# Heron's step for the reciprocal deviation, b2 moved between engines, and later loads, in a conditional residual adapter

## The chip, the cores and the metric

The kernel runs on one core of one Trainium2 chip. The metric is the device time of one execution in microseconds (us). Five engines of the core have queues of their own: TensorE (PE in the profile, and PEld for its weight loads), VectorE (DVE), ScalarE (ACT), GpSimd (POOL), and SyncE (SP), which here only issues DMAs. They run side by side and wait for each other through semaphores.

## What is computed

For each of 128 batches a language id picks one of ten sets of weights. With x of 128 rows and 512 columns per batch, all in fp32:

```python
h = jax.nn.relu(jnp.einsum('bsh,bha->bsa', x, W1[ids]) + b1[ids][:, None, :])   # 512 -> 128
adapted = jnp.einsum('bsa,bah->bsh', h, W2[ids]) + b2[ids][:, None, :]          # 128 -> 512
y = x + adapted
mean = jnp.mean(y, axis=-1, keepdims=True)
var = jnp.mean(jnp.square(y - mean), axis=-1, keepdims=True)
normed = (y - mean) * jax.lax.rsqrt(var + 1e-5)
out = x + normed * gamma[ids][:, None, :] + beta[ids][:, None, :]
```

## The kernel before

**Tiles.** One batch is one tile of 128 rows by 512 columns. x is loaded in groups of G = 4 batches (1 MB) into four buffers (`xp`). All of W1 and W2 stays in SBUF. At the start the ten rows of beta, gamma and b2 are spread over the 128 partitions by small products with a matrix `pick` of ones and zeros (`spread`), into `beta_b`, `gamma_b` and `b2_b`.

**One batch** goes through these steps. TensorE transposes x in four pieces into PSUM (`transpose_x`, L197) and ScalarE copies the result to SBUF (`copy_xT`, L201). ScalarE copies the batch's W1 into one of three buffers (`stage_w1`, L192). TensorE multiplies (`down`, L220), ScalarE applies b1 and relu (`relu`, L228), and TensorE multiplies by W2 (`up`, L237) into y, which has five PSUM buffers (`p_y`). VectorE adds the residual in place and takes the row sums (`residual`, L243), makes the negative mean (L248), later subtracts it and multiplies by gamma (`scale`, L287), and last multiplies by the reciprocal deviation and adds the rest (`finish`, L296), into `o`, which SyncE stores two batches at a time (`store`, L300). ScalarE takes the squares and their sum (`square`, L255) and, for two batches at a time, the root (`deviation`, L261).

**The reciprocal deviation** for two batches is made by five narrow VectorE operations, `rstd_1` to `rstd_5` (L266 to L281): the reciprocal of ScalarE's root, and one Newton step on it.

**b2 and beta.** GpSimd prepares x + b2 (`add_b2`, L207, into `r` of four buffers) and x + beta (`add_beta`, L214, into `o`). For the first four batches and each fourth after them (b % 4 == 1) TensorE adds b2 instead: `up` starts with a product of `pick` and the rows (L236), and the residual is x itself. So GpSimd has seven operations in four batches.

**The order** is written out by hand: the function `keep` ties each instruction to the one before it on its engine, so that each queue runs in program order. Iteration i transposes batch i, multiplies down batch i-1 and up batch i-2 (U = 2), and VectorE works on batch b = i-3 and the pair before it: in even b residual, scale, mean, `rstd_1`, `rstd_2`, finish of batch b-3, `rstd_3`; in odd b residual, `rstd_4`, scale, `rstd_5`, mean, finish of b-3. Each engine that needs language ids loads four of them into registers every fourth batch (`lid`, L174), ahead of use. The load of the group three ahead stands at the top of iterations with i % 4 == 0 (L462) and waits on SyncE's queue until all readers of its buffer are done. At the start up(2) is placed at i = 4 by hand (L465). The last four batches, 124 to 127, go through `tail`, which has an order of its own and gives part of the finish of three batches to ScalarE and GpSimd (`by_pool`); E = 123.

Of the kernel before, what the change touches and what calls it, by code (L numbers as in the profile page):

```python
# [8 lines left out]
FP = mybir.dt.float32  # L9
# [14 lines left out]
def cond_resid_kernel(ctx: ExitStack, tc: tile.TileContext, x, itok, W1, b1, W2, b2, gamma, beta, out):  # L24
# [45 lines left out]
    def xb(b):  # L70
        return xs[b // G][:, b % G, :]
# [55 lines left out]
    both = st.tile([P, R], FP, tag="both", name="both", bufs=1)[:96, :]  # L127
    keep(nc.vector.tensor_tensor(both, ident[:96, 0:R], ident[:96, 32 : 32 + R], ALU.add))
    keep(nc.vector.tensor_tensor(pick, both, ident[:96, 64 : 64 + R], ALU.add))


    wrap = const.tile([1, B], I32, name="wrap")
# [51 lines left out]
        return lids[g, engine][b % G]  # L184

    def b2_by_matmul(b):
        return b < 4 or b % 4 == 1

    def stage_w1(b):
        w1s[b] = wp.tile([P, KC, A], FP, tag="w1s", name=f"w1s_{b}")  # L190
# [10 lines left out]
        keep(nc.scalar.copy(xT[b], pxs.pop(b)))  # L201

    def add_b2(b):
        if not b2_by_matmul(b):
            rs[b] = rp.tile([P, H], FP, tag="r", name=f"r_{b}")
            v = lid(b, ET.Pool)
            keep(nc.gpsimd.tensor_tensor(rs[b], xb(b), b2_b[:, bass.ds(v * H, H)], ALU.add))  # L207
# [22 lines left out]
    def up(b):  # L230
# [6 lines left out]
        keep(nc.tensor.matmul(ys[b], lhsT=hT[b], rhs=w2[:, bass.ds(v * H, H)], start=not m, stop=True))  # L237
        del hT[b]

    def residual(b):  # L240
        r = xb(b) if b2_by_matmul(b) else rs.pop(b)
        s = st.tile([P, 1], FP, tag="sum", name=f"sum_{b}")
        keep(nc.vector.scalar_tensor_tensor(ys[b], ys[b], 1.0, r, ALU.mult, ALU.add, accum_out=s))  # L243
        sums[b] = s

    def negative_mean(b):
        nmeans[b] = st.tile([P, 1], FP, tag="nmean", name=f"nmean_{b}")
        keep(nc.vector.tensor_scalar(nmeans[b], sums.pop(b), -1.0 / H, None, ALU.mult))  # L248

    def square(b):  # L250
        g, j = divmod(b, 2)
        if j == 0:
            ssqs[g] = st.tile([P, 2], FP, tag="ssq", name=f"ssq_{g}")
        sq = tp.tile([P, H], FP, tag="sq", name=f"sq_{b}")
        keep(nc.scalar.activation(sq, ys[b], AF.Square, bias=nmeans[b], accum_out=ssqs[g][:, j : j + 1]))  # L255

    sds, y0s, stats = {}, {}, {}

    def deviation(g):
        sds[g] = st.tile([P, 2], FP, tag="sd", name=f"sd_{g}")  # L260
        keep(nc.scalar.activation(sds[g], ssqs[g], AF.Sqrt, bias=eps, scale=1.0 / H))  # L261


    def rstd_1(g):
        stats[g] = p_s.tile([P, 6], FP, tag="s", name=f"stat_{g}")
        keep(nc.vector.tensor_scalar(stats[g][:, 0:2], ssqs.pop(g), -0.5 / H, -0.5 * EPS, ALU.mult, ALU.add))  # L266

    def rstd_2(g):
        y0s[g] = st.tile([P, 2], FP, tag="y0", name=f"y0_{g}")
        keep(nc.vector.reciprocal(y0s[g], sds.pop(g)))  # L270

    def rstd_3(g):
        keep(nc.vector.tensor_tensor(stats[g][:, 2:4], stats[g][:, 0:2], y0s[g], ALU.mult))  # L273

    def rstd_4(g):
        keep(nc.vector.tensor_tensor(stats[g][:, 4:6], stats[g][:, 2:4], y0s[g], ALU.mult))  # L276

    def rstd_5(g):
        rstds[g] = st.tile([P, 2], FP, tag="rstd", name=f"rstd_{g}")
        keep(  # L280
            nc.vector.scalar_tensor_tensor(rstds[g], stats.pop(g)[:, 4:6], 1.5, y0s.pop(g), ALU.add, ALU.mult)  # L281
        )

    def scale(b):
        v = lid(b, ET.DVE)
        keep(
            nc.vector.scalar_tensor_tensor(  # L287
                ys[b], ys[b], nmeans.pop(b), gamma_b[:, bass.ds(v * H, H)], ALU.add, ALU.mult
            )
        )  # L290

# [11 lines left out]
    def on(b):  # L303
        return 0 <= b < B
# [6 lines left out]
    def rstd_of(b, n):  # L311

        if not ends:
            ends["t"] = p_s.tile([P, 32], FP, tag="s", name="stat_ends")
        t = ends["t"][:, 8 * (b % 4) : 8 * (b % 4) + 3]
        if n == 1:
            keep(nc.vector.tensor_scalar(t[:, 0:1], ssqs.pop(b), -0.5 / H, -0.5 * EPS, ALU.mult, ALU.add))  # L317
        elif n == 2:
            y0s[b] = st.tile([P, 1], FP, tag="y0", name=f"y0_{b}")
            keep(nc.vector.reciprocal(y0s[b], sds.pop(b)))  # L320
        elif n < 5:
            keep(nc.vector.tensor_tensor(t[:, n - 2 : n - 1], t[:, n - 3 : n - 2], y0s[b], ALU.mult))  # L322
        else:
            rstds[b] = st.tile([P, 1], FP, tag="rstd", name=f"rstd_{b}")
            keep(nc.vector.scalar_tensor_tensor(rstds[b], t[:, 2:3], 1.5, y0s.pop(b), ALU.add, ALU.mult))  # L325

    def deviation_of(b):
        ssq = st.tile([P, 1], FP, tag="ssq", name=f"ssq_{b}")
        sq = tp.tile([P, H], FP, tag="sq", name=f"sq_{b}")
        keep(nc.scalar.activation(sq, ys[b], AF.Square, bias=nmeans[b], accum_out=ssq))  # L330
        sds[b] = st.tile([P, 1], FP, tag="sd", name=f"sd_{b}")
        keep(nc.scalar.activation(sds[b], ssq, AF.Sqrt, bias=eps, scale=1.0 / H))
        ssqs[b] = ssq

    def rstd_col(b):
        return rstds[b] if b > E else rstds[b // 2][:, b % 2 : b % 2 + 1]

    def shift(b):
        ends[b] = st.tile([P, 1], FP, tag="shift", name=f"shift_{b}")
        keep(nc.vector.tensor_tensor(ends[b], nmeans.pop(b), rstd_col(b), ALU.mult))  # L340

    def by_pool(b, scaled):

# [16 lines left out]
    def tail(b):  # L360
        p = E // 2
        if b == E + 3:
            rstd_of(b - 2, 4)
        residual(b)
        if b == E + 1:
            rstd_1(p)
            rstd_2(p)
            negative_mean(b)
            rstd_3(p)
            scale(E - 1)  # L370
            rstd_4(p)
            rstd_5(p)
            shift(E)
            finish(E - 2)
            store(p - 1)
            deviation_of(b)
            by_pool(E, False)
        elif b == E + 2:
            negative_mean(b)
            rstd_of(b - 1, 1)  # L380
            rstd_of(b - 1, 2)
            finish_last(E - 1)
            store_last(E)
# [181 lines left out]
```

## Time and profile before

| | us |
|---|---|
| median of 3 runs (319.55 to 320.61) | 319.67 |
| the profiled execution | 319.72 |
| its span (first to last instruction) | 318.0 |
| TensorE multiplies, busy | 302.7 |
| VectorE, busy | 297.9 |
| ScalarE, busy | 289.1 |
| GpSimd, busy | 280.6 |

The granted TensorE clock is 0.99 of full speed in the mean. The profile holds each instruction with its start and duration. Records on VectorE, ScalarE and TensorE overlap with the next one, since an instruction can begin before its forerunner has written its last result; the time that one really takes up on its engine is therefore read from start to start. A line of a timeline gives start, duration, engine, line, operation, what is written and read, shapes, and in brackets the idle time before it with what ended it. A line of the waits gives who waited for whom, the total in us, how often, and the longest.

### The profile page before, as it was taken

The numbers are of one execution on the slowest core, as the hardware profiler recorded it, in microseconds if no ns is written. First come the engines' busy times: TensorE is split into PE (matmuls) and PEld (weight loads), VectorE is DVE, ScalarE is ACT, GpSimd is POOL, SyncE is SP. The second block draws the span as 40 slices with busy tenths as digits, with TensorE's granted clock in tenths as the row PEclk, the third lists the DMA queues.
The fourth block names the chain that finished last, engine by engine and source line by source line (L and its number), as shares of the span: only waits on it lengthen the run. The fifth ranks groups of instructions, "written<-read, shape, count | busy, mean of one in ns | idle before, by whom it ended". The sixth has DMA issues, their size and how long they took to land. (4 is left out here: it accounts for less than half of the span.)

```text
span 318.0 us, 7173 instructions
## 1 busy us (share of the span) xinstructions
PE 302.7 (95%) x1883; PEld 225.0 (71%) x1884; DVE 297.9 (94%) x995; ACT 289.1 (91%) x726; POOL 280.6 (88%) x234
## 2 busy tenths in 40 slices
PE   7989999999999999999999999999999999999950
PEld 3566777777777777777777777777777777777730
DVE  6827999999999999999999999999999999999995
ACT  3977999999999999999999999999999999999971
POOL 1308999999999999999999999999999999999873
PEclk9999999999999999999999999999999999999995
DMA  7998777667776666677776666677766666633333
GB/s 204 318 386 294 205 260 262 233 232 266 260 242 212 215 223 242 228 238 265 261 231 215 209 227 248 223 245 264 258 220 208 222 231 241 219 128 133 132 128 138
DMA packets 41002, 72.88 MB, mean 229 GB/s; under 512 B 1753, under 2 KB 6884, under 8 KB 40962
## 3 DMA queue, kind: packets, MB, share of 16 engines
q1 hardware_dynamic: 40902, 72.38, 67.2%
q8 instruction: 15, 0.25, 0.3%
q14 instruction: 25, 0.20, 0.2%
q10 hardware_dynamic: 60, 0.05, 0.1%
HBM read 38.86 MB, written 33.55 MB: 228 GB/s over the span
## 5 line engine op out<-in xcount | busy, mean ns | idle before, releaser
L214 POOL TENSOR_TENSOR o<-x,beta_b 128x512 f32<-128x512 f32 x128 | 162.1, 1280 | 9.2 <-ACT beta_b L164 9.2
L207 POOL TENSOR_TENSOR r<-x,b_b 128x512 f32<-128x512 f32 x93 | 118.9, 1279 | 20.2 <-DMA x<-in_x_dram 12.3
L220 PE MATMUL ph<-xT,w1s 128*128 128x128 f32 x1024 | 135.6, 275 | 0.7 <-ACT w1s L192 0.5
L237 PE MATMUL py<-w,hT 128*128 x256 | 131.0, 594 | 0.9 <-DMA w<-in_L_cond_W_dram 0.7
L220 PEld LDWEIGHTS ph<-xT,w1s 128*128 128x128 f32 x1024 | 124.6, 192 | 2.8 <-ACT hT L228 1.4
L197 PEld LDWEIGHTS pxT<-ident,x 128*128 128x128 f32 x512 | 63.7, 140 | 66.1 <-issue 45.3
L287 DVE SCALAR_TENSOR_TENSOR py<-py,nmean,gamma_b 128x512 f32<-128x512 f32 x126 | 94.6, 751 | 0.0
L255 ACT ACTIVATE sq<-py,nmean 128x512 f32<-128x512 f32 x124 | 85.3, 688 | 6.7 <-DVE nmean L248 4.2
L296 DVE SCALAR_TENSOR_TENSOR o<-py,rstd,o 128x512 f32<-128x512 f32 x122 | 90.3, 740 | 1.0
L192 ACT COPY w1s<-w 128x512 f32 x128 | 79.5, 622 | 0.2 <-DMA w<-in_L_cond_W_dram 0.2
L201 ACT COPY xT<-pxT 128x512 f32<-128x512 f32 x128 | 73.8, 577 | 5.1 <-PE pxT L197 3.6
L197 PE MATMUL pxT<-ident,x 128*128 128x128 f32 x512 | 76.8, 273 | 0.7 <-ACT xT L201 0.7
L243 DVE SCALAR_TENSOR_TENSOR py<-py,r 128x512 f32<-128x512 f32 x93 | 64.4, 692 | 2.5 <-PE pxT L197 0.9
L228 ACT ACTIVATE hT<-ph,b1T 128x128 f32<-128x128 f32 x128 | 47.6, 372 | 1.2 <-PE ph L220 1.2
L237 PEld LDWEIGHTS py<-w,hT 128*128 128x128 f32 x256 | 41.6, 192 | 4.0 <-issue 2.0
L243 DVE SCALAR_TENSOR_TENSOR py<-py,x 128x512 f32<-128x512 f32 x35 | 24.1, 690 | 4.9 <-PE py L237 4.8
L255 ACT ACTIVATION_READ_ACCUMULATOR sq<-py,nmean 128x1 f32 x124 | 24.8, 200 | 0.0
L261 ACT ACTIVATE sd<-ssq,eps 128x2 f32<-128x2 f32 x62 | 18.3, 296 | 2.1
L248 DVE TENSOR_SCALAR nmean<-sum 128x1 f32<-128x1 f32 x128 | 18.7, 146 | 0.2
L236 PE MATMUL py<-parts,pick 96*128 96x512 bf16 x35 | 13.3, 381 | 0.0
L243 DVE DVE_READ_ACCUMULATOR py<-py,r 128x1 f32 x93 | 13.0, 140 | 0.0
L276 DVE TENSOR_TENSOR stat<-stat,y 128x2 f32<-128x2 f32 x62 | 12.7, 205 | 0.0
(54 smaller groups left out, 113.7 us busy)
## 6 DMA issues: line engine op xcount, KB each, us to landing
out_dram<-o SPq DMA_DIRECT2D x61, 512.0 KB, 3.6
x<-in_x_dram SPq DMA_DIRECT2D x30, 1024.0 KB, 6.0
w<-in_L_cond_W_dram SPq DMA_DIRECT2D x4, 640.0 KB, 6.6
w<-in_L_cond_W_dram SPq DMA_DIRECT2D x2, 1280.0 KB, 11.3
x<-in_x_dram SPq DMA_DIRECT2D x4, 512.0 KB, 8.5
out_dram<-o SPq DMA_DIRECT2D x6, 256.0 KB, 2.4
rows<-in_L_cond_beta_dram ACTq DMA_DIRECT2D x1, 20.0 KB
rows<-in_L_cond_gamma_dram SPq DMA_DIRECT2D x1, 20.0 KB
```

The costliest lines, as they stand in the source:

```text
L192: keep(nc.scalar.copy(w1s[b].rearrange("p k a -> p (k a)"), src))
L197: keep(nc.tensor.transpose(pxs[b][:, k, :], xb(b)[:, k * P : (k + 1) * P], ident))
L201: keep(nc.scalar.copy(xT[b], pxs.pop(b)))
L207: keep(nc.gpsimd.tensor_tensor(rs[b], xb(b), b2_b[:, bass.ds(v * H, H)], ALU.add))
L214: keep(nc.gpsimd.tensor_tensor(os[g][:, j, :], xb(b), beta_b[:, bass.ds(v * H, H)], ALU.add))
L220: nc.tensor.matmul(phs[b], lhsT=w1s[b][:, k, :], rhs=xT[b][:, k, :], start=(k == 0), stop=(k == KC - 1))
L228: keep(nc.scalar.activation(hT[b], phs.pop(b), AF.Relu, bias=b1T[:, bass.ds(lid(b, ET.Activation), 1)]))
L237: keep(nc.tensor.matmul(ys[b], lhsT=hT[b], rhs=w2[:, bass.ds(v * H, H)], start=not m, stop=True))
L243: keep(nc.vector.scalar_tensor_tensor(ys[b], ys[b], 1.0, r, ALU.mult, ALU.add, accum_out=s))
L255: keep(nc.scalar.activation(sq, ys[b], AF.Square, bias=nmeans[b], accum_out=ssqs[g][:, j : j + 1]))
L287: nc.vector.scalar_tensor_tensor(ys[b], ys[b], nmeans.pop(b), gamma_b[:, bass.ds(v * H, H)], ALU.add, ALU.mult)
L296: nc.vector.scalar_tensor_tensor(o, ys.pop(b), rstds[g][:, j : j + 1], o, ALU.mult, ALU.add)
```

## The change

- **The reciprocal deviation** takes four narrow operations in place of five. With s the root and v the variance (each with its constants), it forms 1/s, v/s, v/s + s, and the reciprocal of that, which is half of the wanted 1/deviation; the factor 2 goes into gamma, by doubling gamma's columns of `pick` once at the start. `square` computes (sum - 512 y)^2, so its bias is the sum and not the mean; the constants of the root follow (1/H^3).
- **The order of VectorE's narrow operations**: `rstd_1` moves ahead of scale in even batches, `rstd_5` and its place are gone, so that `rstd_4` stands ahead of scale in odd ones. `tail` is ordered anew.
- **b2**: batches with b % 8 == 5 from 13 to 109 no longer have it from TensorE; VectorE adds it to y in place with a tensor_tensor ahead of the residual. GpSimd's share is unchanged.
- **Loads of x** stand at b % 4 == 0, three iterations later, when their buffer is free.
- **up(3)** is issued at the top of iteration 5, ahead of transposes(5) and down(4), in place of its end.
- The last additions of GpSimd, after batch 123, alternate.
- Sums and means of two batches share a tile.

```diff
+    keep(nc.vector.tensor_scalar(pick[:, L : 2 * L], pick[:, L : 2 * L], 2.0, None, ALU.mult))
...
     def b2_by_matmul(b):
-        return b < 4 or b % 4 == 1
+        return b < 4 or (b % 4 == 1 and not b2_by_vector(b))
+
+    def b2_by_vector(b):
+        return b % 8 == 5 and 8 <= b < B - 16
...
     def residual(b):
...
+        if b2_by_vector(b):
+            v = lid(b, ET.DVE)
+            keep(nc.vector.tensor_tensor(ys[b], ys[b], b2_b[:, bass.ds(v * H, H)], ALU.add))
+        keep(
+            nc.vector.scalar_tensor_tensor(ys[b], ys[b], 1.0, r, ALU.mult, ALU.add, accum_out=col(sums, b))
+        )
...
     def square(b):
...
-        keep(nc.scalar.activation(sq, ys[b], AF.Square, bias=nmeans[b], accum_out=ssqs[g][:, j : j + 1]))
+        keep(
+            nc.scalar.activation(
+                sq, ys[b], AF.Square, bias=col(sums, b), scale=-float(H), accum_out=col(ssqs, b)
+            )
+        )
...
     def rstd_1(g):
+        y0s[g] = p_s.tile([P, 6], FP, tag="s", name=f"stat_{g}")
+        keep(nc.vector.reciprocal(y0s[g][:, 0:2], sds[g]))
 
     def rstd_2(g):
+        t = y0s[g]
+        keep(nc.vector.scalar_tensor_tensor(t[:, 2:4], ssqs.pop(g), EPS * H3, t[:, 0:2], ALU.add, ALU.mult))
 
     def rstd_3(g):
+        t = y0s[g]
+        keep(nc.vector.scalar_tensor_tensor(t[:, 4:6], t[:, 2:4], 1.0 / H3, sds.pop(g), ALU.mult, ALU.add))
 
     def rstd_4(g):
         rstds[g] = st.tile([P, 2], FP, tag="rstd", name=f"rstd_{g}")
+        keep(nc.vector.reciprocal(rstds[g], y0s.pop(g)[:, 4:6]))
...
     def tail(b):
         p = E // 2
         if b == E + 3:
-            rstd_of(b - 2, 4)
+            rstd_of(b - 2, 3)
         residual(b)
         if b == E + 1:
             rstd_1(p)
+            scale(E - 1)
             rstd_2(p)
             negative_mean(b)
-            rstd_3(p)
-            scale(E - 1)
-            rstd_4(p)
-            rstd_5(p)
-            shift(E)
             finish(E - 2)
             store(p - 1)
+            rstd_3(p)
             deviation_of(b)
+            rstd_4(p)
+            shift(E)
             by_pool(E, False)
         elif b == E + 2:
+            rstd_of(b - 1, 1)
             negative_mean(b)
-            rstd_of(b - 1, 1)
             rstd_of(b - 1, 2)
             finish_last(E - 1)
             store_last(E)
-            rstd_of(b - 1, 3)
             deviation_of(b)
         elif b == E + 3:
-            rstd_of(b - 2, 5)
-            negative_mean(b)
+            rstd_of(b - 2, 4)
             shift(b - 2)
             residual(b + 1)
-            negative_mean(b + 1)
             by_pool(b - 2, False)
             store_last(b - 2)
             rstd_of(b - 1, 1)
+            negative_mean(b)
             rstd_of(b - 1, 2)
-            rstd_of(b - 1, 3)
+            negative_mean(b + 1)
             scale(b - 1)
             deviation_of(b)
+            rstd_of(b - 1, 3)
             rstd_of(b - 1, 4)
-            rstd_of(b - 1, 5)
             scale(b)
             deviation_of(b + 1)
             by_pool(b - 1, True)
             store_last(b - 1)
             rstd_of(b, 1)
             rstd_of(b, 2)
             rstd_of(b + 1, 1)
+            rstd_of(b, 3)
             rstd_of(b + 1, 2)
-            rstd_of(b, 3)
-            rstd_of(b + 1, 3)
             scale(b + 1)
             rstd_of(b, 4)
+            rstd_of(b + 1, 3)
             rstd_of(b + 1, 4)
-            rstd_of(b, 5)
-            rstd_of(b + 1, 5)
             finish_last(b)
             finish_last(b + 1)
...
     for i in range(3, B + U):
-        if i < B and i % G == 0 and i // G + 3 < NG:
-            load_x(i // G + 3)
         b = i - U - 1
+        if b > 0 and b % G == 0 and b // G + 3 < NG:
+            load_x(b // G + 3)
         if i == 4:
             up(2)
+        if i == 5:
+            up(3)
...
-        if i > 4 and on(i - U):
+        if i > 5 and on(i - U):
             up(i - U)
...
         if b == E:
-            for n in range(b + 3, B):
-                add_b2(n)
-            for n in range(b + 1, B):
+            add_b2(b + 3)
+            add_beta(b + 1)
+            add_b2(b + 4)
+            for n in range(b + 2, B):
                 add_beta(n)
...
             if mine:
+                rstd_1(p)
                 scale(2 * p)
             if on(b):
                 negative_mean(b)
             if mine:
-                rstd_1(p)
                 rstd_2(p)
...
                 rstd_4(p)
                 scale(2 * p + 1)
-                rstd_5(p)
```

More of the change, by code (lines that the diff above doesn't have):

```diff
@@ L203, in add_b2 @@
     def add_b2(b):
-        if not b2_by_matmul(b):
+        if not b2_by_matmul(b) and not b2_by_vector(b):
             rs[b] = rp.tile([P, H], FP, tag="r", name=f"r_{b}")
@@ L238, in up, with col @@
         del hT[b]
+    def col(tiles, b):
+        return tiles[b // 2][:, b % 2 : b % 2 + 1]
     def residual(b):
[L241 to L244, printed above, removed]
+        r = rs.pop(b) if b in rs else xb(b)
+        if b % 2 == 0:
+            sums[b // 2] = st.tile([P, 2], FP, tag="sum", name=f"sum_{b // 2}")
+        if b2_by_vector(b):
[4 more added lines that the diff above has]
+        )
     def negative_mean(b):
-        nmeans[b] = st.tile([P, 1], FP, tag="nmean", name=f"nmean_{b}")
-        keep(nc.vector.tensor_scalar(nmeans[b], sums.pop(b), -1.0 / H, None, ALU.mult))
+        if b % 2 == 0:
+            nmeans[b // 2] = st.tile([P, 2], FP, tag="nmean", name=f"nmean_{b // 2}")
+        keep(nc.vector.tensor_scalar(col(nmeans, b), col(sums, b), -1.0 / H, None, ALU.mult))
     def square(b):
@@ L254, in square @@
         sq = tp.tile([P, H], FP, tag="sq", name=f"sq_{b}")
-        keep(nc.scalar.activation(sq, ys[b], AF.Square, bias=nmeans[b], accum_out=ssqs[g][:, j : j + 1]))
+        keep(
[3 more added lines that the diff above has]
+        )
     sds, y0s, stats = {}, {}, {}
+    H3 = float(H) ** 3
     def deviation(g):
         sds[g] = st.tile([P, 2], FP, tag="sd", name=f"sd_{g}")
-        keep(nc.scalar.activation(sds[g], ssqs[g], AF.Sqrt, bias=eps, scale=1.0 / H))
+        keep(nc.scalar.activation(sds[g], ssqs[g], AF.Sqrt, bias=eps, scale=1.0 / H3))
     def rstd_1(g):
-        stats[g] = p_s.tile([P, 6], FP, tag="s", name=f"stat_{g}")
-        keep(nc.vector.tensor_scalar(stats[g][:, 0:2], ssqs.pop(g), -0.5 / H, -0.5 * EPS, ALU.mult, ALU.add))
+        y0s[g] = p_s.tile([P, 6], FP, tag="s", name=f"stat_{g}")
+        keep(nc.vector.reciprocal(y0s[g][:, 0:2], sds[g]))
     def rstd_2(g):
-        y0s[g] = st.tile([P, 2], FP, tag="y0", name=f"y0_{g}")
-        keep(nc.vector.reciprocal(y0s[g], sds.pop(g)))
+        t = y0s[g]
+        keep(nc.vector.scalar_tensor_tensor(t[:, 2:4], ssqs.pop(g), EPS * H3, t[:, 0:2], ALU.add, ALU.mult))
     def rstd_3(g):
-        keep(nc.vector.tensor_tensor(stats[g][:, 2:4], stats[g][:, 0:2], y0s[g], ALU.mult))
+        t = y0s[g]
+        keep(nc.vector.scalar_tensor_tensor(t[:, 4:6], t[:, 2:4], 1.0 / H3, sds.pop(g), ALU.mult, ALU.add))
     def rstd_4(g):
-        keep(nc.vector.tensor_tensor(stats[g][:, 4:6], stats[g][:, 2:4], y0s[g], ALU.mult))
-    def rstd_5(g):
         rstds[g] = st.tile([P, 2], FP, tag="rstd", name=f"rstd_{g}")
-        keep(
-            nc.vector.scalar_tensor_tensor(rstds[g], stats.pop(g)[:, 4:6], 1.5, y0s.pop(g), ALU.add, ALU.mult)
-        )
+        keep(nc.vector.reciprocal(rstds[g], y0s.pop(g)[:, 4:6]))
     def scale(b):
@@ L287, in scale @@
             nc.vector.scalar_tensor_tensor(
-                ys[b], ys[b], nmeans.pop(b), gamma_b[:, bass.ds(v * H, H)], ALU.add, ALU.mult
+                ys[b], ys[b], col(nmeans, b), gamma_b[:, bass.ds(v * H, H)], ALU.add, ALU.mult
             )
@@ L316, in rstd_of @@
         if n == 1:
-            keep(nc.vector.tensor_scalar(t[:, 0:1], ssqs.pop(b), -0.5 / H, -0.5 * EPS, ALU.mult, ALU.add))
+            keep(nc.vector.reciprocal(t[:, 0:1], sds[b]))
         elif n == 2:
[L319 to L322, printed above, removed]
+            keep(
+                nc.vector.scalar_tensor_tensor(t[:, 1:2], ssqs.pop(b), EPS * H3, t[:, 0:1], ALU.add, ALU.mult)
+            )
+        elif n == 3:
+            keep(nc.vector.scalar_tensor_tensor(t[:, 2:3], t[:, 1:2], 1.0 / H3, sds.pop(b), ALU.mult, ALU.add))
         else:
             rstds[b] = st.tile([P, 1], FP, tag="rstd", name=f"rstd_{b}")
-            keep(nc.vector.scalar_tensor_tensor(rstds[b], t[:, 2:3], 1.5, y0s.pop(b), ALU.add, ALU.mult))
+            keep(nc.vector.reciprocal(rstds[b], t[:, 2:3]))
     def deviation_of(b):
@@ L329, in deviation_of @@
         sq = tp.tile([P, H], FP, tag="sq", name=f"sq_{b}")
-        keep(nc.scalar.activation(sq, ys[b], AF.Square, bias=nmeans[b], accum_out=ssq))
+        keep(nc.scalar.activation(sq, ys[b], AF.Square, bias=col(sums, b), scale=-float(H), accum_out=ssq))
         sds[b] = st.tile([P, 1], FP, tag="sd", name=f"sd_{b}")
-        keep(nc.scalar.activation(sds[b], ssq, AF.Sqrt, bias=eps, scale=1.0 / H))
+        keep(nc.scalar.activation(sds[b], ssq, AF.Sqrt, bias=eps, scale=1.0 / H3))
         ssqs[b] = ssq
@@ L339, in shift @@
         ends[b] = st.tile([P, 1], FP, tag="shift", name=f"shift_{b}")
-        keep(nc.vector.tensor_tensor(ends[b], nmeans.pop(b), rstd_col(b), ALU.mult))
+        keep(nc.vector.tensor_scalar(ends[b], col(nmeans, b), rstd_col(b), None, ALU.mult))
     def by_pool(b, scaled):
```

## The prediction, made before the changed kernel ran

> **What bounds the kernel now.** I read the page's first part, then the waits of the middle of the run (50 to 290 us), the timelines of TensorE and VectorE, and last the register loads. Four engines are above 88% busy, so shares decide nothing:
>
> ```profile
> PE 302.7 (95%) x1883; PEld 225.0 (71%) x1884; DVE 297.9 (94%) x995; ACT 289.1 (91%) x726; POOL 280.6 (88%) x234
> ```
>
> The waits of the middle, the whole list of those of 2 us and more:
>
> ```profile
> PEld pxT L197 <- issue: 39.4, 143, 0.3
> PEld pxT L197 <- ACT w1s L192: 13.2, 55, 0.2
> POOL r L207 <- DVE py L243: 6.5, 22, 0.6
> PEld pxT L197 <- ACT xT L201: 3.6, 14, 0.4
> ACT sq L255 <- DVE nmean L248: 2.0, 10, 0.3
> ```
>
> TensorE's multiply (PE) is not in it at all; PEld is only the weight load under it, 0.2 to 0.3 us of it per batch whatever it is put down to. GpSimd and ScalarE each wait a little, for others. The timeline of TensorE, between two b2 products:
>
> ```profile
> 149.98 0.38 PE L236 MATMUL py<-parts,pick 96*128 96x512 bf16 x1
> 150.20 1.02 PE L237 MATMUL py<-w,hT 128*128 x2
> ...
> 154.58 1.02 PE L237 MATMUL py<-w,hT 128*128 x2
> 156.77 1.02 PE L237 MATMUL py<-w,hT 128*128 x2
> 158.96 0.38 PE L236 MATMUL py<-parts,pick 96*128 96x512 bf16 x1
> ```
>
> The up products stand 2.19 us apart, and the b2 product (L236) moves the one behind it by 0.22 (150.20-149.98), so four batches take 4x2.19+0.22 = 8.98. Its starts lie 8.98 or 8.99 apart all the way from 42 to 303 us, but for one 9.21. **TensorE sets the pace.** VectorE is almost as late. Its timeline from the scale of an odd batch to the next residual, start and duration first:
>
> ```profile
> 201.44 0.75 DVE L287 SCALAR_TENSOR_TENSOR py<-py,nmean,gamma_b 128x512 f32<-128x512 f32 x1
> 202.10 0.15 DVE L281 SCALAR_TENSOR_TENSOR rstd<-stat,y 128x2 f32<-128x2 f32 x1
> 202.17 0.15 DVE L248 TENSOR_SCALAR nmean<-sum 128x1 f32<-128x1 f32 x1
> 202.29 0.75 DVE L296 SCALAR_TENSOR_TENSOR o<-py,rstd,o 128x512 f32<-128x512 f32 x1
> 203.09 0.70 DVE L243 SCALAR_TENSOR_TENSOR py<-py,r 128x512 f32<-128x512 f32 x1
> ```
>
> Records overlap, so I count from start to start. Averages over 70 to 290 us: residual 0.61, scale 0.66, finish 0.65 to 0.67, a narrow operation 0.06 to 0.07. Two things are dearer: from the mean (L248) to finish takes 0.146 in odd batches, since finish needs rstd_5's result from two places ahead; and every second odd finish is followed by 0.80 (202.29 to 203.09) in place of 0.67. There the registers of the next four batches are loaded (0.61 us on VectorE's sequencer, begun at 202.30):
>
> ```profile
> L174 DVEq TENSOR_LOAD <-lang x32: 341/612/1049, 24.6 to 301.0; - x32
> ```
>
> The odd batch is 2.22, the even one 2.18: 4.40 a pair, 8.81 for four, and 8.94 with the load's 0.13. So VectorE needs 8.94 of TensorE's 8.98. Relief of TensorE alone would be worth 0.04 per four batches. ScalarE needs 8.60 (4.30 a pair where it doesn't wait), GpSimd 7x1.232 = 8.62.
>
> **What the Trainium skill says.** "VectorE: DVE Perf Modes", section on the TRN2 errata: an fp32 tensor_tensor takes (N+151)/0.96 ns, 691 at N = 512. The trace has none of that size from PSUM; its residual, the same operands, takes 0.69. "PSUM — Partial Sum Buffer", section "Engine vs sequencer instructions": a sequencer instruction waits until those before it are dispatched, not finished. The trace agrees: the register load starts 0.01 after finish does. "TensorE: Matmul & The Clock Gate", section "Back-to-back issue gap": N/2.4+2.5 ns, 216 for 512 columns; the trace has 0.22 for the b2 product.
>
> **The change part by part.** The sum stands against the profiled execution, 319.72 us (span 318.0 and 1.7 around it), 0.05 over the median 319.67.
>
> *TensorE, b2.* Batches 13, 21, ... 109 lose their b2 product: 13 x 0.22 = **2.86** on the path, if VectorE keeps up. Eight batches then take TensorE 8x2.19+0.22 = 17.74 where it was 17.96.
>
> *VectorE.* Four narrow operations for five, and rstd_4 now lies a scale ahead of finish, so the 0.08 wait goes. Odd: residual 0.61, rstd_4 0.07, scale 0.66, mean 0.065, finish 0.665 = 2.07. Even: 0.61, rstd_1 0.065, scale 0.66, mean 0.06, rstd_2 0.065, finish 0.65, rstd_3 0.065 = 2.175. A pair is 4.245; eight batches are 16.98 and one added tensor_tensor. That one: at least a residual's step, 0.61; at most its whole duration and the 0.04 that a directly dependent narrow operation shows behind its forerunner's end (24.60 to 24.64), since residual reads its result: 0.73, which I take. The register load costs 0 to 0.13 twice. I take 0: finish's wait is now over while scale still runs, so by the quoted section the load can start under scale. Sum 17.71 (17.59 to 17.97) against 17.74. The vector batch puts VectorE some 0.6 late, and it regains that over the next seven. Who waits behind the added instruction: finish of the same turn, thus TensorE's up two batches on, which needs that buffer of y. In the trace finish(b-3) ends at 153.80 and 155.91, the up it frees starts at 154.58 and 156.77: slack 0.8, with VectorE about 0.2 late already. So 0.6 fits. ScalarE's square needs only the sum now, not the mean 0.73 later, which absorbs the same lateness. rstd_1 moves ahead of scale, and scale now waits for ScalarE's root: that ends at 154.15 for a residual started at 153.72, so rstd_1 would come at 154.33; room 0.18, and if gone VectorE stalls only while it is early.
>
> *Loads of x.* On SP's queue a load moves behind one store. Now it is issued 0.3 after the residual that frees its buffer (152.27), then at about 156.3, behind the store at 155.94: 4 us later. It lands in 6 us (median), and is needed by the transposes some 11 batches, 24 us, later. Cost 0, and no gain: the load waits only 0.4 there now, and the store behind it comes 3.7 later. Without the cover each us of lateness would be a us on TensorE. The first load waits for its buffer until 30.5 as before.
>
> *Fourth up first.* At the start TensorE stands 0.68 idle at 26.33 for ScalarE's copy of xT(4), and up(3), 1.08, comes only at 28.40. Ahead of transposes(5) it fills that gap. By TensorE's own order transposes(6) come at 28.57 for 29.48 (0.91). But down(5) needs its one buffer of ph from relu(4), which ScalarE ends at about 29.25, so down(5) starts at 29.3 for 29.91: **0.58** (0 to 0.91). VectorE follows: residual(3) need no longer wait 1.25 at 29.68.
>
> *Tail.* From residual(124) at 301.73 to the last end at 314.52 VectorE runs 12.79: it is the whole chain.
>
> ```profile
> 303.44 0.16 DVE L276 TENSOR_TENSOR stat<-stat,y 128x2 f32<-128x2 f32 x1
> 303.62 0.16 DVE L281 SCALAR_TENSOR_TENSOR rstd<-stat,y 128x2 f32<-128x2 f32 x1
> 303.82 0.46 DVE L340 TENSOR_TENSOR shift<-nmean,rstd 128x1 f32<-128x1 f32 x1
> 304.20 0.74 DVE L296 SCALAR_TENSOR_TENSOR o<-py,rstd,o 128x512 f32<-128x512 f32 x1
> ...
> 313.11 1.41 DVE L357 SCALAR_TENSOR_TENSOR o<-py,rstd,o 128x512 f32<-128x512 f32 x2 [0.39 <-issue]
> ```
>
> A directly dependent narrow step costs 0.19 (303.44 to 303.62) in place of 0.065. Twelve wide operations (four each of residual, scale, finish) are 7.76; 31 narrow ones and their gaps take 5.03. After: the same wide ones, 26 narrow, of which by the new order 7 follow their source directly: 19x0.065+7x0.19 = 2.57; 0.26 waiting for ScalarE's root of batch 127 and 0.14 for y of 126 and 127; and 0.39 if the unexplained gap at 313.11 stays: 3.36. Gain 1.67 (1.2 to 2.2), and 0.13 since residual(124) comes less late: **1.8**. The stores behind it move along. GpSimd's reordered last additions fill its 1.48 wait at 298.06; it isn't on the chain.
>
> *Nothing:* the doubling of gamma's columns is one narrow VectorE operation at 1.9 us, hidden by the 0.36 wait for the rows' DMA (0.2 if not). Square, with its sum as bias, stays one operation with one pointer.
>
> Sum 2.86+0.58+1.8 = 5.24: 319.72-5.24 = **314.5**.
>
> **The rivals.**
> 1. *VectorE becomes the bound* (24%). For: it is at 8.94 of 8.98, and the added operation eats what the shorter chain frees. With 17.97 per eight, TensorE keeps only the lateness that the buffers of y absorb, about 0.4: 319.72-0.4-0.58-1.2 to 1.8, about **317.2** (316 to 319). Against: the load's place.
> 2. *The ends give nothing* (10%): ScalarE, back to back from 26.4, and gaps as that at 313.11 take the place of what is removed; only 2.86 and some 0.4: **316.4**.
> 3. *Slower* (6%): the added operation with its dependent residual stalls VectorE more than any row shows. To outweigh the ends, 2.4, eight batches must take 17.96+2.4/13 = 18.14, thus operation and load stalls 1.16 where the rows bound 0.99. From there each 0.1 costs 1.3; at 1.5 it gives **324**. The place would be finish in batches 13, 21, ..., and TensorE's L237 waiting for it.
>
> **How the numbers follow.** The forecast, TensorE still the bound, has 60%; its own range is 313.3 (0.91 at the start, 2.35 at the tail, and the one turn of 9.21 back to 8.98) to 315.7 (0 and 1.2). The range reaches into rivals 1 and 2: 313.3 to 317.3, leaving out the slower end of 1 and all of 3. A measurement of this kernel tells about 0.3% (1 us) from no change. Faster: 0.60+0.10 and three quarters of rival 1, 0.88; within: the rest of it, 0.06; slower 0.06.
>
> **What would show it.** TensorE's b2 starts 17.74 apart between 60 and 270 us confirm the first term; 17.8 or more with L237 waiting for finish is rival 1. VectorE's pair without the added operation should be 4.25, the added step 0.73, the register load should start under scale. down(5) should start near 29.3; VectorE's tail should take about 11.1. A pair above 4.35, or an added step above 0.9, makes the prediction wrong.

## The result, and the profile after

| | us |
|---|---|
| before, median of 6 runs (319.53 to 320.61) | 319.67 |
| changed, median of 6 runs (313.95 to 314.64) | 314.19 |
| ratio, with its 95% interval | 0.9825 [0.9812, 0.9838] |
| predicted | 314.5 (313.3 to 317.3) |
| the profiled execution of the changed kernel, and its span | 314.2, 312.4 |

The kernel became 5.5 us faster. In experiment 8 three of the six runs took over 1.5% more than the fastest, at a slightly lower granted clock, and its figures are those of the other three.

The first line of the changed kernel's page answers the one shown of before:

```profile
PE 300.3 (96%) x1870; PEld 222.8 (71%) x1871; DVE 295.6 (95%) x943; ACT 285.8 (91%) x726; POOL 280.1 (90%) x234
```

TensorE has 13 products fewer, VectorE 52 instructions fewer (the narrow ones) although 13 wide ones came in. Shares again decide nothing: VectorE's rose from 94% to 95% of a shorter span. The waits of the middle (50 to 290 us; who waited for whom, total, times, longest):

```profile
PEld pxT L202 <- issue: 40.4, 147, 0.3
PEld pxT L202 <- ACT w1s L197: 16.0, 67, 0.2
ACT xT L206 <- PE pxT L202: 4.2, 14, 0.3
POOL r L212 <- DVE stat L289: 3.4, 8, 0.5
```

Still no row in which PE waits, and ScalarE's wait for the mean (2.0 before) is gone. TensorE's timeline from one b2 product to the next:

```profile
183.41 0.38 PE L241 MATMUL py<-parts,pick 96*128 96x512 bf16 x1
183.63 1.02 PE L242 MATMUL py<-w,hT 128*128 x2
...
201.16 0.38 PE L241 MATMUL py<-parts,pick 96*128 96x512 bf16 x1
```

201.16-183.41 = 17.75, against two turns of 8.98 before: TensorE goes on without a gap, one product lighter. VectorE's timeline of an odd batch, and the changed kernel's row of register loads:

```profile
171.70 0.69 DVE L257 SCALAR_TENSOR_TENSOR py<-py,r 128x512 f32<-128x512 f32 x1
172.30 0.14 DVE L257 DVE_READ_ACCUMULATOR py<-py,r 128x1 f32 x1
172.30 0.17 DVE L301 RECIPROCAL rstd<-stat 128x2 f32<-128x2 f32 x1
172.39 0.74 DVE L306 SCALAR_TENSOR_TENSOR py<-py,nmean,gamma_b 128x512 f32<-128x512 f32 x1
173.03 0.15 DVE L263 TENSOR_SCALAR nmean<-sum 128x1 f32<-128x1 f32 x1
173.09 0.74 DVE L315 SCALAR_TENSOR_TENSOR o<-py,rstd,o 128x512 f32<-128x512 f32 x1
173.75 0.69 DVE L257 SCALAR_TENSOR_TENSOR py<-py,r 128x512 f32<-128x512 f32 x1
```
```profile
L176 DVEq TENSOR_LOAD <-lang x32: 348/820/1416, 24.4 to 296.7; - x32
```

Read from start to start: mean to finish is 0.06 where it was 0.146 on average, and finish to the next residual 0.66 where before it was 0.80 in a turn with a register load. This turn has one too: it starts at 172.59, under scale, and lasts 0.82. It has become longer and costs nothing here. Two loads in this execution did cost something. The worse one starts at 57.28, lasts 1.42, and holds the residual back:

```profile
57.78 0.74 DVE L315 SCALAR_TENSOR_TENSOR o<-py,rstd,o 128x512 f32<-128x512 f32 x1
58.86 0.70 DVE L257 SCALAR_TENSOR_TENSOR py<-py,r 128x512 f32<-128x512 f32 x1 [0.34 <-issue]
```

Finish to residual is 1.08 there in place of 0.66. VectorE was still late from it at the next addition (batch 21), and TensorE's products up of batches 23 and 24 came another 0.08 and 0.10 late, so that one turn of eight batches took 17.93 in place of 17.74. The added operation and the residual behind it look like this:

```profile
175.94 0.69 DVE L255 TENSOR_TENSOR py<-py,b_b 128x512 f32<-128x512 f32 x1
176.66 0.70 DVE L257 SCALAR_TENSOR_TENSOR py<-py,x 128x512 f32<-128x512 f32 x1
```

From start to start it takes 0.72.

Where the 5.52 us of the two spans (317.96 and 312.44) went, stage by stage, from the starts of b2 products (of batches 1, 5 and 113), of residual(124), and the ends of the last finish and of the span:

| stage | gained | forecast |
|---|---|---|
| start: the rows of W2 landed earlier in the changed kernel's execution | 0.23 | none |
| start: the fourth product up | 0.47 | 0.58 |
| middle: b=5 to b=113 | 2.88 | 2.86 |
| residual(124) less late | 0.12 | 0.13 |
| tail, residual(124) to the end of the last finish (12.79 to 11.47) | 1.32 | 1.67 |
| last finish to the end of the span, the last store (3.44 to 2.94) | 0.49 | none |

The first and the last row belong to these two executions and not to the change. Experiment 2 starts and ends with the code of before, and has batch 1's b2 at 23.36 and 2.93 behind its last finish; experiment 12 has the changed start and the changed loads and stores, with 24.04 and 3.40. The middle has one longer turn in each trace, 9.21 for 8.98 before and 17.93 for 17.74 after; with both taken off it gives 2.84.

### The profile page after: what moved, and what is told of

Same layout as the page of the kernel before. It is cut to its first block, busy times and chain, and to the rows that moved or that the text cites. A ratio compares the mean times of both kernels' runs of the same rounds, so it can differ in the third digit from the quotient of the medians.

```text
span 312.4 us, 7096 instructions
## 1 busy us (share of the span) xinstructions
PE 300.3 (96%) x1870; PEld 222.8 (71%) x1871; DVE 295.6 (95%) x943; ACT 285.8 (91%) x726; POOL 280.1 (90%) x234
## 4 chain that ended last, share of the span: by engine, by line
PE 84%; DVE 4%; DMA 4%; SPq 3%; ACT 2%; issue 1%; DVEq 1%; ACTq 0%
PE ph L225 34%; PE py L242 33%; PE pxT L202 17%; DMA w<-in_L_cond_W_dram 4%; SPq L98 2%; PE py L241 1%; DVE py L257 1%; DVE py L306 1%; SPq L84 1%; DVE o L315 1%; ACT sq L350 0%; DVEq L577 0%; ACT xT L206 0%; ACT n L366 0%; ACT sq L272 0%
## 5 line engine op out<-in xcount | busy, mean ns | idle before, releaser
L306 DVE SCALAR_TENSOR_TENSOR py<-py,nmean,gamma_b 128x512 f32<-128x512 f32 x126 | 93.6, 743 | 0.0
L272 ACT ACTIVATE sq<-py,sum 128x512 f32<-128x512 f32 x124 | 85.2, 687 | 2.0 <-DVE py L257 1.8
L242 PEld LDWEIGHTS py<-w,hT 128*128 128x128 f32 x256 | 40.5, 192 | 3.2 <-issue 1.6
L272 ACT ACTIVATION_READ_ACCUMULATOR sq<-py,sum 128x1 f32 x124 | 25.6, 207 | 0.0
L263 DVE TENSOR_SCALAR nmean<-sum 128x1 f32<-128x1 f32 x128 | 19.4, 151 | 0.1
L289 DVE RECIPROCAL stat<-sd 128x2 f32<-128x2 f32 x62 | 12.9, 208 | 1.1 <-ACT sd L283 1.1
L301 DVE RECIPROCAL rstd<-stat 128x2 f32<-128x2 f32 x62 | 10.3, 167 | 0.0
```

What stands on the lines that cost most here:

```text
L272: nc.scalar.activation(sq, ys[b], AF.Square, bias=col(sums, b), scale=-float(H), accum_out=col(ssqs, b))
L306: nc.vector.scalar_tensor_tensor(ys[b], ys[b], col(nmeans, b), gamma_b[:, bass.ds(v * H, H)], ALU.add, ALU.mult)
```

## The experiments

The theory: TensorE stays the bound by 0.04 of 17.74 us, because the shorter chain and the hidden register load pay for the added operation; the rest comes from the two ends. The rivals: VectorE has become the bound, or the gain lies only in the ends or only in b2.

**1. All but the move of b2** (no_b2). `b2_by_vector` returns False.

> The changed kernel with TensorE adding b2 in every fourth batch again; the rest of the change stays. Theory (the sum): TensorE sets the pace in both, so the 13 products of 0.22 us come back: its b2 starts stand 8.98 apart and the time is 314.2+2.9, about 317.0. VectorE then has slack, 2x8.49 = 16.97 in 17.96, and its residual starts at the least lateness in nearly every batch. Rival (the gain of the middle comes from VectorE's shorter chain, not from TensorE's): the time stays near 314.2 and the b2 starts stand closer than 8.98.

Measured 317.7, ratio 0.9927 [0.9908, 0.9946]. The b2 starts are 8.98 apart everywhere, and in all batches of the middle but two (1.18 and 1.31) residual starts at most 1.17 behind its product up: VectorE only waits for TensorE. In this execution W2's rows came later (TensorE waits 0.8 for that DMA in place of 0.5, and batch 1's b2 stands at 23.88 in place of 23.35), which is a part of the excess over the expectation. From the b2 product of batch 5 to that of batch 113 it takes 242.49, which is what the kernel before takes without its one longer turn (242.72-0.23). The changed kernel takes 239.84, or 239.65 without its stalled turn. So the move of b2 is worth 2.84 in the middle, and the shorter chain by itself nothing there.

**2. Only the move of b2, on the kernel before** (b2_alone).

```diff
-        return b < 4 or b % 4 == 1
+        return b < 4 or (b % 4 == 1 and not b2_by_vector(b))
...
+            keep(nc.vector.tensor_tensor(ys[b], ys[b], b2_b[:, bass.ds(v * H, H)], ALU.add))
```

> The kernel before with one part of the change alone: VectorE adds b2 in batches 13, 21, ... 109. Theory: VectorE, which needs 2x8.94 = 17.88 for eight batches there, needs 17.88+0.72 = 18.60 and becomes the bound; TensorE, which could do 17.74, waits in L237 for finish. From 17.96 to 18.60 is 0.64 a turn, 13 turns 8.3, less some 0.5 that the buffers of y absorb: about 327.5 us. Rival (TensorE's relief is worth its 2.9 by itself): about 317.

Measured 327.68 (two runs), ratio 1.0235 [1.0184, 1.0286], with b2 starts 18.6 apart. In its waits of the middle there is what the changed kernel lacks:

```profile
PEld py L240 <- DVE o L302: 6.0, 13, 0.8
PE py L240 <- DVE o L302: 3.5, 12, 0.6
```

TensorE's product up waits for the finish that frees its y, in 12 or 13 places. The same edit costs 8 us with the five narrow operations in their old order, and gains 2.8 with the four in the new one. This is rival 1's mechanism, and it shows how near it lay.

**3. rstd_4 behind scale in odd batches** (rstd4_late), as rstd_5 stood before: the finish again depends on something two places ahead.

```diff
-                rstd_4(p)
                 scale(2 * p + 1)
+                rstd_4(p)
```

> The changed kernel with rstd_4 behind the scale of the odd batch in place of ahead of it; nothing else. Theory: finish then waits for rstd_4 again (0.085 a pair), and the register load of each fourth batch, held behind finish, costs 0.13 again. Eight batches of VectorE: 17.70+4x0.085+2x0.13 = 18.30 against TensorE's 17.74; 13 turns of 0.56 less 0.5 absorbed: about 314.2+6.8 = 321. Rival (the place of one narrow operation is worth only its own step, and VectorE has room): within 0.5 of 314.2.

Measured 324.3 (two runs), ratio 1.0129 [1.0081, 1.0177]: the mechanism that was expected, at a higher price. Eight batches take 18.48 (18.30 expected). VectorE's timeline in a turn with a load:

```profile
205.54 0.76 DVE L306 SCALAR_TENSOR_TENSOR py<-py,nmean,gamma_b 128x512 f32<-128x512 f32 x1
206.20 0.16 DVE L301 RECIPROCAL rstd<-stat 128x2 f32<-128x2 f32 x1
206.28 0.13 DVE L263 TENSOR_SCALAR nmean<-sum 128x1 f32<-128x1 f32 x1
206.40 0.75 DVE L315 SCALAR_TENSOR_TENSOR o<-py,rstd,o 128x512 f32<-128x512 f32 x1
207.23 0.70 DVE L257 SCALAR_TENSOR_TENSOR py<-py,r 128x512 f32<-128x512 f32 x1
```

Mean to finish is 0.12 here and 0.15 in the mean; the load starts 0.01 behind finish, and finish to residual is 0.83. As the prediction read from "PSUM — Partial Sum Buffer", section "Engine vs sequencer instructions", of the Trainium skill, a sequencer instruction goes once those ahead are dispatched: one narrow operation in the wrong place holds finish back, finish the load, and the load the next residual.

**4. VectorE adds b2 in each fourth batch** (all_vec): `return b % 4 == 1 and 8 <= b < B - 16`.

> The changed kernel with VectorE adding b2 in every fourth batch from 9 to 109, TensorE in none of them. Theory: TensorE could do eight batches in 8x2.19 = 17.52, but VectorE needs 16.97+2x0.724 = 18.42 and becomes the bound: 13 turns of 18.42-17.74 = 0.68, less 0.5 absorbed, about 314.2+8.3 = 322.5, and TensorE waits in L242 for finish. Rival (there is still room on VectorE; more relief of TensorE gives more): 314.2-2.9, about 311.4.

Measured 322.25, ratio 1.0073 [1.0051, 1.0095]. 108 batches take 247.75, 18.35 for eight; by VectorE's rows four pairs and two additions are 4x4.245+2x0.73 = 18.44, so they price it to 0.1. The waits of the middle:

```profile
PEld py L242 <- DVE o L315: 9.1, 25, 0.4
PE py L242 <- DVE o L315: 4.3, 24, 0.2
```

**5. up(3) late, as before** (up3_late): the two lines of i == 5 taken out, `i > 5` back to `i > 4`.

> The changed kernel with up(3) back at the end of iteration 5. Theory: TensorE stands 0.68 for the copy of xT(4) again, and the fifth down starts about 0.57 later; the product of b2 in batch 5 comes about 0.5 later, and all that follows by as much: about 314.7. Rival (ScalarE sets the pace at the start, so the place of up(3) is hidden): no difference, 314.2.

Measured 314.72 (314.46 to 314.83), ratio 0.9835 [0.9817, 0.9853]. In its trace the b2 products of batches 1 and 5 lie 9.42 apart, in the changed kernel's 8.95: 0.47.

**6. Loads of x in their old place** (old_loads).

> The changed kernel with the loads of x back at the top of every fourth iteration. Theory: the loads are issued up to 4 us earlier, and nothing waits for either: 314.2, within 0.3 per cent. Rival (a load that waits on SyncE's queue holds back the store behind it, and so the end): slower by some tenths, above all where GpSimd is late at the start.

Measured 314.0 (313.97 to 314.08), ratio 0.9812 [0.9794, 0.9830]. Moving the loads is worth nothing that can be measured.

**7. The old order of the tail, with the four narrow operations** (old_tail).

> The changed kernel with the order of the last four batches as before (four narrow operations for five, but each where it stood). Theory: more narrow operations follow their source directly, 11 for 7, 0.125 each, 0.5 in all, and finish(121) comes later, which holds up(126): the last finish ends about 12.1 behind the start of residual(124) where the changed kernel takes 11.47, and the time is about 314.9. Rival (the gain of the tail comes from the missing operations alone): 314.2 to 314.4.

Measured 315.0 (314.39 to 315.02), ratio 0.9838 [0.9819, 0.9857]. The first and the last line of its tail on VectorE:

```profile
297.96 0.70 DVE L257 SCALAR_TENSOR_TENSOR py<-py,r 128x512 f32<-128x512 f32 x1
...
308.54 1.41 DVE L377 SCALAR_TENSOR_TENSOR o<-py,rstd,o 128x512 f32<-128x512 f32 x2
```

From 297.96 to 309.95 it is 11.99: of the 1.32 gained in the tail, 0.52 is the order. The other 0.80 is not the missing operations alone. The kernel before had a gap of 0.39 ahead of its last finishes, here it is 0.04. Experiment 2, whose tail has the code of before, doesn't have that gap either (its last two reciprocal deviations, then its last two finishes):

```profile
321.12 0.22 DVE L331 SCALAR_TENSOR_TENSOR rstd<-stat_ends,y 128x1 f32<-128x1 f32 x2
321.37 1.41 DVE L363 SCALAR_TENSOR_TENSOR o<-py,rstd,o 128x512 f32<-128x512 f32 x2
```

The gap is 0.03 there, so the old code by itself doesn't make it. (The tail of experiment 2 still takes 12.69, since residual(127) comes 0.24 later in it.) And `shift`, which the change also turns from a tensor_tensor into a tensor_scalar, takes 0.13 from its start to the next where it took 0.38 and 0.15. That is 0.35 for the gap and 0.27 for the two shifts; some 0.2 is left for the missing operations and all else.

**8. One negative mean for two batches** (pair_mean), to take a further narrow operation off VectorE: in odd batches a 128x2 tensor_scalar in place of two of 128x1.

```diff
+        if b <= E:
+            if b % 2 == 1:
+                keep(nc.vector.tensor_scalar(nmeans[b // 2], sums[b // 2], -1.0 / H, None, ALU.mult))
+            return
         keep(nc.vector.tensor_scalar(col(nmeans, b), col(sums, b), -1.0 / H, None, ALU.mult))
```

> The changed kernel with one negative mean for two batches, made in the odd one, up to batch 123: 0.061 less per pair, so VectorE needs about 17.46 for eight batches in place of 17.70. Theory: TensorE's 17.74 is the bound, so nothing moves: b2 starts 17.74 apart and 314.2. Only the lateness of VectorE falls by 0.28 in eight batches in place of 0.04. Rival (VectorE is the bound at 17.70 to 17.74): b2 starts closer together, down to 17.5, and up to 3 us less, about 311.

Measured 353.08 (350.09 to 354.97), ratio 1.1015 [1.0949, 1.1081]. Neither theory had that. Its timelines, first VectorE's, then GpSimd's in the same stretch:

```profile
203.50 0.73 DVE L310 SCALAR_TENSOR_TENSOR py<-py,nmean,gamma_b 128x512 f32<-128x512 f32 x1
204.15 1.11 DVE L265 TENSOR_SCALAR nmean<-sum 128x2 f32<-128x2 f32 x1
205.17 0.74 DVE L319 SCALAR_TENSOR_TENSOR o<-py,rstd,o 128x512 f32<-128x512 f32 x1
```
```profile
203.97 1.27 POOL L212 TENSOR_TENSOR r<-x,b_b 128x512 f32<-128x512 f32 x1
205.19 2.50 POOL L219 TENSOR_TENSOR o<-x,beta_b 128x512 f32<-128x512 f32 x2
```

The operation on 256 numbers takes 1.11 and ends at 205.26; GpSimd's addition, begun 0.18 ahead of it, ends at 205.24. Five microseconds later it is the same: 210.18 and 210.15. One waited through three additions:

```profile
45.56 3.34 DVE L265 TENSOR_SCALAR nmean<-sum 128x2 f32<-128x2 f32 x1
```

All 62 of these means end 0.02 to 0.03 behind the end of an addition of GpSimd. In 13 of them that addition was nearly over, and they took 0.16 to 0.18; the others took 0.88 to 1.16, but for the one of 3.34. From 70 to 290 us the step is 0.74 on average, where the 128x1 form takes 0.06. The Trainium skill has a cause that fits: by "VectorE: DVE Perf Modes", section "What auto-detection actually checks", an instruction with a single source goes into a two-port form if source and result are in SBUF and their outermost dimensions above one are both even or equal; by "SBUF — State Buffer", section "Who interferes with whom", the second pair of ports is GpSimd's too, and whoever comes second waits for the whole instruction of the other. The ends in the trace agree to 0.03, though the page doesn't say that one can wait through three in a row. Experiments 9 and 12 test the cause.

**9. The pair's mean with its result in PSUM** (pair_mean_psum). By the first page cited in 8, this takes the two-port form away; it leaves the place and the count. The two columns are put into the PSUM tile that holds the reciprocals.

```diff
...
+                y0s[b // 2] = p_s.tile([P, 8], FP, tag="s", name=f"stat_{b // 2}")
+                nmeans[b // 2] = y0s[b // 2][:, 6:8]
...
```

> The pair's one negative mean (128x2) again, at the same place in the order, but written to two columns of the PSUM tile that holds the root's reciprocals. If it was the two SBUF ends of that instruction that made it wait for GpSimd's running addition, it now takes a step of 0.07 like the narrow operations beside it; VectorE then needs 17.74-4x0.06 = 17.5 per eight batches, TensorE's 17.74 stays the bound, and the time is that of the changed kernel, 314.2 (b2 starts 17.74 apart). If making the mean late, for two batches at once, is what hurt, it stays near 355.

Measured 340.92 (340.63 to 341.31), ratio 1.065 [1.063, 1.067]. Half of the expectation held. VectorE's timeline:

```profile
201.26 0.75 DVE L311 SCALAR_TENSOR_TENSOR py<-py,stat,gamma_b 128x512 f32<-128x512 f32 x1
202.04 0.16 DVE L267 TENSOR_SCALAR stat<-sum 128x2 f32<-128x2 f32 x1
202.13 0.75 DVE L320 SCALAR_TENSOR_TENSOR o<-py,rstd,o 128x512 f32<-128x512 f32 x1
...
203.40 0.21 DVE L294 RECIPROCAL stat<-sd 128x2 f32<-128x2 f32 x1
203.65 0.76 DVE L311 SCALAR_TENSOR_TENSOR py<-py,stat,gamma_b 128x512 f32<-128x512 f32 x1
204.44 0.17 DVE L298 SCALAR_TENSOR_TENSOR stat<-ssq,stat 128x2 f32<-128x2 f32 x1
```

The mean takes 0.16 and its step 0.08 to 0.09: the wait for GpSimd is gone. But its neighbours have become dear: scale to mean 0.78 (0.65 in the changed kernel), rstd_1 to scale 0.24 (0.08), scale to rstd_2 0.80 (0.65 from scale to whatever follows it in the changed kernel). Each starts 0.03 to 0.04 behind the end of its forerunner, as an instruction does that reads its forerunner's result. None of them reads it. Two of them only use other columns of the same tile than their forerunner; the mean writes into the pool's one buffer for these tiles, over the columns that the scale ahead of it has read. A pair takes 4.72 (4.245 in the changed kernel), and eight batches 19.6.

**10 and 11. More batches by VectorE, on the same kernel** (psum_more: `b % 8 == 5 and b < 120`; psum_five: `b % 32 in (5, 13, 17, 25, 29) and b < 120`).

> The pair's mean in PSUM, and VectorE adds b2 in two batches more, 5 and 117. TensorE as the bound: two products of 0.22 fewer, 314.2-0.44 = 313.8. If VectorE, at 17.5 of 17.74 per eight batches, can't regain the last addition's 0.73 ahead of batch 124, the tail gives it back: 314.2.

> The pair's mean in PSUM, and VectorE adds b2 in five of eight of the batches with b % 4 == 1, from 5 to 117 (18 in place of 13). Per 32 batches TensorE then takes 32x2.19+3x0.22 = 70.7 and VectorE 16x4.18+5x0.73 = 70.5. TensorE as the bound: 314.2-5x0.22 = 313.1. If two additions four batches apart make VectorE later than the buffers of y cover (its residual more than about 2.2 behind the product up), each such place costs some 0.1: 313.6.

Measured 342.51, ratio 1.0701 [1.0679, 1.0723], and 344.67, ratio 1.0762 [1.0742, 1.0782]. Their condition, TensorE as the bound, didn't hold, so they don't answer their question. What they tell: with VectorE as the bound two more additions cost 1.6 and five 3.75, 0.75 to 0.8 each, the whole step of 0.72 and nothing hidden.

**12. Both causes of 8 and 9 avoided, five of eight by VectorE, own tiles in the tail** (best).

```diff
...
+                    nc.vector.scalar_tensor_tensor(
+                        nmeans[b // 2], sums[b // 2], -1.0 / H, y1s[b // 2 - 1], ALU.mult, ALU.bypass
+                    )
...
-        return b % 8 == 5 and 8 <= b < B - 16
+        return b % 32 in (5, 13, 17, 25, 29) and b < 120
...
-            ends["t"] = p_s.tile([P, 32], FP, tag="s", name="stat_ends")
+            pool, tag = {0: (p_s, "s"), 1: (p_s, "s"), 2: (p_h, "h"), 3: (p_x, "xT")}[b % 4]
+            ends["t", b] = pool.tile([P, 3], FP, tag=tag, name=f"stat_{b}")
```

> Three edits on the changed kernel, each of which shows in its own place. (1) The pair's negative mean as a scalar_tensor_tensor whose second operand, which it passes over, is in PSUM, and whose result stays in SBUF in a tile of its own: no two-port form, and no wait for a neighbour in the same tile. If these two were what cost pair_mean and pair_mean_psum their time, its step is 0.065 and a pair without an added b2 4.18; else again 4.6 or more. (2) VectorE adds b2 in five of eight of the batches with b % 4 == 1 from 5 on (18 in place of 13): TensorE 70.7 per 32 batches, VectorE 70.5; worth 5x0.22 = 1.1. (3) In the tail the reciprocals of each of the last batches have a PSUM tile of their own, in banks that the transposes and the product down have done with: three steps of 0.2 that wait for a neighbour's result become 0.07, worth 0.4 on a tail of 11.47. Together 314.2-1.1-0.4 = 312.7; 313.2 if two additions four batches apart make TensorE wait.

Measured 313.87 (313.82 to 314.31), ratio 0.9801 [0.9786, 0.9816]. That is 0.3 below the changed kernel's median, but the two intervals overlap, so the runs don't tell the two kernels apart; the stages of the traces do. The pair's mean:

```profile
296.60 0.74 DVE L317 SCALAR_TENSOR_TENSOR py<-py,nmean,gamma_b 128x512 f32<-128x512 f32 x1
297.25 0.15 DVE L266 SCALAR_TENSOR_TENSOR nmean<-sum,stat 128x2 f32<-128x2 f32 x1
297.32 0.74 DVE L326 SCALAR_TENSOR_TENSOR o<-py,rstd,o 128x512 f32<-128x512 f32 x1
```

Its step is 0.063, scale to mean 0.647, a pair 4.18 in the median (4.18 expected): with two sources, one of them in PSUM, and a tile of its own, both penalties are gone, so pairing the means was never what hurt. It also answers what experiment 8 asked. Where only one of eight batches has the addition, VectorE now needs 4x4.18+0.72 = 17.44, and the b2 products still lie 17.74 to 17.75 apart: TensorE is the bound.

From batch 1's b2 product to batch 117's TensorE takes 257.16 (257.76 in the changed kernel, of which 0.19 is its stalled turn): 0.41 of the 1.1 hoped for. The other 0.7 goes in the seven places where two additions lie four batches apart, about 0.1 in each. TensorE's product up and the finish that frees its buffer of y:

```profile
88.29 1.02 PE L242 MATMUL py<-w,hT 128*128 x2
90.48 1.12 PE L242 MATMUL py<-w,hT 128*128 x2
92.77 1.02 PE L242 MATMUL py<-w,hT 128*128 x2
```
```profile
89.68 0.75 DVE L326 SCALAR_TENSOR_TENSOR o<-py,rstd,o 128x512 f32<-128x512 f32 x1
```

That finish ends at 90.43, the product starts at 90.48, takes 1.12 in place of 1.02, and the next comes 2.29 later in place of 2.19: 0.10, too short for the list of waits. VectorE's residual is 2.16 behind its product after such a pair of additions, 1.88 in the changed kernel's steady turns; twelve batches with a pair of additions take 26.60 where their products sum to 26.50. The tail gives 0.45, 11.02 in place of 11.47; the same stretch on VectorE, in the changed kernel and then in this one:

```profile
306.40 0.17 DVE L336 RECIPROCAL stat_ends<-sd 128x1 f32<-128x1 f32 x1
306.60 0.17 DVE L342 SCALAR_TENSOR_TENSOR stat_ends<-stat_ends,sd 128x1 f32<-128x1 f32 x1
306.81 0.16 DVE L339 SCALAR_TENSOR_TENSOR stat_ends<-ssq,stat_ends 128x1 f32<-128x1 f32 x1
```
```profile
306.36 0.17 DVE L348 RECIPROCAL stat<-sd 128x1 f32<-128x1 f32 x1
306.44 0.15 DVE L354 SCALAR_TENSOR_TENSOR stat<-stat,sd 128x1 f32<-128x1 f32 x1
306.57 0.16 DVE L351 SCALAR_TENSOR_TENSOR stat<-ssq,stat 128x1 f32<-128x1 f32 x1
```

The three steps belong to two batches in turn. 0.20 and 0.21 became 0.08 and 0.13. The two batches' tiles are now in different PSUM buffers, and the pair's mean has left PSUM; so whether steps are tied by the tile or by the part of PSUM that it lies in, and whether by the chip or by a wait that the program sets, no run shows. Against 0.60+0.45 stands that in this execution W2's rows landed later (batch 1's b2 at 24.04 in place of 23.35) and the end behind the last finish took 3.40 in place of 2.94.

## Why the prediction was right

- **TensorE stays the bound, 2.86.** Measured 2.88, or 2.84 without the one longer turn in each trace, which experiment 1 repeats. Eight batches are 17.74 as forecast, but for one turn of 17.93. This was the likeliest case, and the forecast of 314.5 is 0.3 above the median.
- **VectorE's sum, 17.71.** Its pair is 4.243 (4.245 forecast), the added step 0.724 (0.73 forecast, the upper of the two bounds), the operation itself 0.69 long: 17.70. The lower bound, a residual's 0.61, would have been wrong. VectorE's lateness shows it: in the steady turns the residual starts 1.14 behind its product, 1.88 in a batch with the addition, and is back at 1.14 when the next addition comes, eight batches later. After the stall at 57 us it comes back by only 0.05 to 0.06 in eight batches, about the margin of 0.04 that the sums give.
- **The register load, 0.** It starts under scale, for the reason that the prediction gave, in nearly every turn. Two stood out: the one of 1.42 at 57.28 cost VectorE 0.42 and TensorE 0.19, and one that started late, at 146.54, cost VectorE 0.24. Experiment 3 puts its price back.
- **Rival 1** was near. Experiments 2, 3 and 4 each push VectorE over 17.74 and land on its mechanism, at 18.35 to 18.6 per eight. That the forecast won by 0.04 in 17.74 was read correctly, but it is a margin that one misplaced narrow operation eats.
- **Loads of x, 0.** Experiment 6 agrees.
- **Fourth product up, 0.58.** Measured 0.47, twice. down(5) started at 29.11 against the 29.3 forecast, but the whole start was 0.23 earlier, for W2's rows. VectorE's residual(3) moved from 29.68 to 28.97.
- **The tail, 1.67, is the mis-sized term: 1.32, and 0.97 without the gap in the kernel before.** The working counted 7 dependent narrow steps at 0.19 and kept the unexplained gap of 0.39 ahead of the last finishes. The gap is gone (finish(126) starts 0.09 after the last rstd_4 starts), but experiment 2 hasn't got it on the old tail either, so some 0.35 of the 1.32 can't be put down to the change; what made the gap no run shows. Without it the working gives 2.97 for everything narrow, and the trace has 11.47-7.76 = 3.71. Of these 0.74, 0.45 go in experiment 12: steps of different batches that share the tile stat_ends are tied like dependent ones, which the count by data left out. The other 0.3 isn't settled. Nor does the working single out `shift`, whose two steps are 0.27 shorter.
- **Luck: 0.49 behind the last finish and 0.23 at W2's rows.** The last store landed 2.0 after its issue in this execution and 2.4 before. Neither was forecast and neither is the change's doing. Together with the gap they make up for what the tail and the start lack, so that the sum of the terms (5.24 forecast, 5.52 between the spans) is nearer than the terms themselves. Without these two and the gap, the two traces show some 4.4 for the change, while the medians of six runs each lie 5.48 apart; how the difference is made up in the other executions isn't known.
- **Rivals 2 and 3.** The ends gave 1.9 by the trace without the two DMAs' shares, and 1.55 without the gap as well, so they did not fall to nothing; the added operation with its load stall costs 0.724, far from the 1.16 of rival 3.

## What to carry to other kernels

When two engines lie within 1% of each other, sum each one's queue from start to start over a whole period, added operations at their full dependent step, and ask what every sequencer instruction stands behind: here the place of one narrow operation turned a gain of 5.5 us into a loss of 4 (experiment 3). Before a narrow VectorE operation is merged or moved beside a busy GpSimd, look at where its operands are: in experiment 8 a 128x2 operation with one source, from SBUF to SBUF, made a step of 0.74 where 0.06 had been. Try tiles of their own, in PSUM buffers of their own, for independent narrow results where a chain of them is the critical path: experiment 12 gained 0.45 of a tail of 11.47 by it. And look at what the same code does in more than one trace before a term of half a microsecond is put down to a change.

## What the hardware showed that was not expected

- A 128x2 tensor_scalar from SBUF to SBUF took about 1.1, once 3.34, and ended with an addition of GpSimd to within 0.03 in all 62 cases (experiment 8); with its result in PSUM it took 0.16, and as a two-source form with one source in PSUM 0.15.
- A wait of the same kind fits a row that the prediction showed without explaining: shift(123) of the kernel before, a tensor_tensor with two sources in SBUF, took 0.46 and ended at 304.28. GpSimd's row of the kernel before, three additions, ends at 304.26:

```profile
300.52 3.74 POOL L214 TENSOR_TENSOR o<-x,beta_b 128x512 f32<-128x512 f32 x3
```

  The other shift of the kernel before and both of experiment 2 end 0.02 to 0.03 behind an addition of GpSimd too. In the changed kernel shift is a tensor_scalar on one column; the one at 303.17 took 0.21, with GpSimd's addition running from 303.07 to 304.34. No run changed the form of shift alone.

- A register load on VectorE's queue lengthened from 0.61 to 0.82 in the median when it moved under scale, and cost nothing there but in two turns of the changed kernel.
- W2's rows land up to 0.7 us apart from one execution to the next (batch 1's b2 product at 23.35, 23.88 and 24.04 in three traces), and all that follows moves with them. The end behind the last finish takes 2.93 to 3.44. Each is as large as what experiments 5 to 7 were to tell apart, so those are read from stages of the trace, not from the span alone.
